# Graph transformer stack on one core: VectorE by hand, deferred statistics, bursts of two or three

## The chip, the cores and the metric

The kernel runs on one core of a Trainium2 chip. The core has five engines with an instruction queue each: TensorE (PE in the profile, its weight loads PEld), VectorE (DVE), ScalarE (ACT), GpSimd (POOL) and SyncE (SP), which issues most DMAs. The metric is the device time of one execution in microseconds (us).

## What is computed

Sixteen graphs of 1024 nodes with 128 features share one adjacency matrix. Three layers of masked attention with eight heads of 16, each followed by a feed-forward part of 256, and a last layer of graph attention with one head. All is float32.

```python
def layer(x):                       # L0, L1, L2: own weights each
    Q, K, V = (h @ Wq), (h @ Wk), (h @ Wv)          # 8 heads of 16
    scores = einsum('bnhd,bmhd->bhnm', Q, K) / sqrt(HEAD_DIM)
    scores = where(adj == 0, -inf, scores)
    attn = softmax(scores, axis=-1)
    attn_out = einsum('bhnm,bmhd->bnhd', attn, V).reshape(B, N, OUT_DIM)
    x = layer_norm(h + (attn_out @ Wo + bo), ln1_g, ln1_b)
    y = relu(x @ W1 + b1) @ W2 + b2
    return layer_norm(x + y, ln2_g, ln2_b)

def last(x):                        # L3
    h = x @ W
    e = leaky_relu((h @ a_src)[:, :, None] + (h @ a_dst)[:, None, :], 0.2)
    att = softmax(where(adj == 0, -inf, e), axis=-1)
    return layer_norm(einsum('bij,bjd->bid', att, h) + x)
```

(Names and numbers of dimensions are shortened; x has 16 x 1024 x 128 values here as the kernel asserts it.)

## The kernel before

**Blocks, steps, pairs.** A block is one graph in one of the three attention layers: 48 blocks, four graphs taken in turn through the layers (`LANES`). A block has 32 steps: two groups of four heads, two halves of 512 queries, eight tiles of 128 keys. A step has two pairs; a pair is the scores of two heads of one tile of keys against 512 queries, 128 x 1024 values in one of three slots `s` of PSUM (two banks each). One bank `t` is for all other products, one, `acc`, for the sums of probabilities and values.

**A pair's way.** TensorE computes the scores (L428). On DVE's way (`on_dve`, L436) VectorE adds the mask on the way out of PSUM (L438) and ScalarE takes the exponential in SBUF one burst later (L473), two pairs in one instruction where they lie side by side. On POOL's way (`on_pool`, L441) ScalarE takes the exponential out of PSUM (L443) and GpSimd multiplies by a mask of zeros and ones (L444). `av_step` (L479) multiplies the probabilities by the values into `acc`; after eight steps `finish` transposes the sums on VectorE into `tt` (L490), takes a reciprocal (L492), and GpSimd scales into `A` (L493).

**Bursts.** The main loop (L836) takes three pairs at a time: `burst` puts the outer two on DVE's way and the middle one on POOL's, in every sixteenth burst all three on DVE's (`POOL_RESTS`). An operation of the graph layer's edges (`fill`, L634, with its VectorE operation L645) makes a burst with one pair on POOL's way. After the burst's scores come: one piece, the exponentials of the burst before, the sums of steps that are three bursts old (`AHEAD`), and a second piece.

**Pieces.** All other work stands in chains of tasks, with the tiles each takes and gives back: the projections of the next block (`proj_tasks`: two transpositions `t0`, four `split`, which leave a rounded part on ScalarE, L392, and the rest on VectorE, L393, and two `v`), what follows a block's attention (`post_tasks`: `gather`, `out_proj`, `x1t`, `ffn1`, `ffn2`), and the graph layer (`last_tasks`: `xt`, `nodes`, `rows_gh`, four times `edges` and `aggregate`, `end`). `AT` gives the step of a block from which each piece of a projection or post chain is due; others are due some steps after the one before. `piece` takes the first due one. `need` forces pieces that must be done. A projection or an FFN product is emptied from `t` on VectorE (L336) and followed by statistics of four tiles (L329, L331) and by GpSimd's normalisation (L344 to L348).

**Who sets the order.** In the main loop TensorE's and ScalarE's instructions stand in the order of the program (`manual_schedule`). VectorE's, GpSimd's and SyncE's stand where a list scheduler puts them by a model of costs; `soon` raises the priority of some evacuations. Each engine then runs its queue in that order, with waits on semaphores. After the last block the remaining chains are run off in the loop at L872.

Of the kernel before, what the change touches and what calls it, by code (L numbers as in the profile page):

```python
# [32 lines left out]
AT = {"proj": (1.5, 4.5, 9, 10.5, 12, 15, 16.5, 18), "post": (13.5, 19.5, 21, 22.5, 24, 25.5, 27, 28.5, 30, 39.5)}  # L33
AT_END = {3: (13.5, 19.5, 21, 22.5, 24, 25.5, 27, 28.5, 30, 31.5), 2: (7.5, 9, 12, 13.5, 15, 16.5, 18, 19.5, 21, 22.5)}
AHEAD = 3
BURST = 3
POOL_RESTS = 16
# [79 lines left out]
def fast_path(ctx: ExitStack, tc: tile.TileContext, a: dict, out: bass.AP, flag):  # L117
# [169 lines left out]

    def transpose_half(name, src, h, gain=None, bias=None):
# [44 lines left out]
    def add_and_stats(n):  # L333
        def out(ts, ps):
            with soon():
                nc.vector.tensor_add(n[0][:, ts, :], v3(ps), n[0][:, ts, :])  # L336
            stats(n, ts)
        return out
# [24 lines left out]

    def proj_tasks(m):
# [4 lines left out]
        def t0(h):  # L369
            def run():  # L370
                x = state["x", b]
                if l == 0:
# [10 lines left out]
        def split(n, h):  # L383
            def run():
# [6 lines left out]
                with soon():  # L391
                    nc.scalar.copy(hi[:, c], ps)  # L392
                    nc.vector.tensor_sub(lo[:, c], ps, hi[:, c].bitcast(F32))  # L393
            return run
# [8 lines left out]
        pieces = [t0(0), t0(1), split("Wk", 0), split("Wq", 0), split("Wk", 1), split("Wq", 1), v(0), v(1)]  # L403
        return [(2 if n in (3, 4, 5, 6) else 1, f, {0: "+w", 1: "+w", 6: "-w", 7: "-w"}.get(n, "")) for n, f in enumerate(pieces)]
# [42 lines left out]
    e_of, masked, bursts = {}, [], [0]  # L447

    def burst(edge, pairs):

        old = list(masked)
        masked.clear()
        if edge is not None:
            edge()
            on_pool(*pairs[0], e_pair())
        else:
            e, ep = e_tile(), e_pair()
            rests = bursts[0] % POOL_RESTS == POOL_RESTS - 1 or len(pairs) < BURST
            for i, pair in enumerate(pairs):
                if i == 1:  # L460
                    (on_dve if rests else on_pool)(*pair, ep)
                else:
                    on_dve(*pair, e[:, i:i + 2, :])
            masked.append(e[:, 0:2 * ((len(pairs) + 1) // 2)])
            if rests and len(pairs) > 1:
                masked.append(ep)
            bursts[0] += 1
# [14 lines left out]
    def finish(g, qh, acc):  # L482

        def run():
# [4 lines left out]
            with soon():  # L489
                nc.vector.transpose(tt.rearrange("p a b -> p (a b)"), acc)  # L490
            rec = state["recs"][:, g, qh, :]
# [6 lines left out]
    def post_tasks(b, l):  # L498
# [4 lines left out]
        def gather(h):  # L503
            def run():
                s["aT", h] = half_tile("aT")
                nc.vector.transpose(s["aT", h], att[:, h].rearrange("p k g d -> p (k g d)"))
                if h == 1:
                    check_range(recs.rearrange("p g h k -> p (g h k)"))
            return run

        def out_proj(h):
            def run():
                if h == 0:
                    s["n1"] = with_stats(state["x", b])
                project([s["aT", h]], [w["Wo"]], h, add_and_stats(s["n1"]))
                normalise(s["n1"], slice(4 * h, 4 * h + 4))
            return run

        def x1t(h, alone=False):
            def run():  # L520
                x1 = s["n1"][0]
# [16 lines left out]
        def ffn2(h):  # L538
            def run():
# [4 lines left out]
                normalise(s["n2"], slice(4 * h, 4 * h + 4))  # L544
# [31 lines left out]
    def last_tasks(b):  # L576
# [3 lines left out]
        def xt(h):  # L580
            def run():
                w = W[L - 1]
                if h == 0:
# [70 lines left out]
        def aggregate(u):  # L654
            def run():
# [13 lines left out]
                stats(s["n"], slice(2 * u, 2 * u + 2))  # L669
                if u % 2:  # L670
                    normalise(s["n"], slice(2 * u - 2, 2 * u + 2))
                if u == 3:
                    check_range(s["col"].rearrange("p c t -> p (c t)"))
            return run

        def end():
            y = s["n"][0]
# [54 lines left out]

    def piece():
# [35 lines left out]
    def av_next():  # L769
# [7 lines left out]
        if left[half] == 0:  # L777
            m, g, qh = half
            b, l = blocks[m]
            while g == 0 and qh == 0 and last_attn:  # L780
                need(last_attn.pop())
            finish(g, qh, sums)()
# [51 lines left out]
    with tc.manual_schedule(engines={mybir.EngineType.PE, mybir.EngineType.Activation}):  # L834
# [278 lines left out]
```

## Time and profile before

| what | us |
|---|---|
| median of three runs | 4096.12 (4089.81 to 4096.95) |
| the profiled execution | 4093.11 |
| its span, first to last instruction | 4091.3 |
| mask additions on VectorE, 2074 | 2423.4, 1211 ns each |
| multiplications on GpSimd, 998 | 2008.6, 2026 ns each |
| exponentials in SBUF on ScalarE, 1068 | 1989.8 |
| exponentials out of PSUM on ScalarE, 998 | 1027.2, 1029 ns each |
| products with the values on TensorE | 1545.7 |
| scores on TensorE | 1096.2 |

A row of a list of groups gives line, engine, operation, tiles and shapes, count, busy time, mean time of one in ns, and the idle time of the engine just before these instructions with what ended it. A row of waits gives the waiting instruction, what released it, the sum in us, how often, and the longest. A row of the timeline gives start, duration in us, engine, line, operation, tiles and count of merged instructions; in brackets the idle time before.

### The profile page before, as it was taken

The page shows a single profiled execution, that of the slowest core. Times are in us where ns is not written, and L with a number is a line of the kernel's source. Part 1 is how long each engine was busy: PE and PEld are TensorE (multiplying, and loading weights), DVE is VectorE, ACT ScalarE, POOL GpSimd, SP SyncE. Part 2 cuts the span into 40 slices and gives each one's busy share as a digit, 9 for nine tenths or more (in the row PEclk, how much of TensorE's full clock was granted, in tenths as well). Part 3 has the DMA queues.
Part 4 walks back from the last instruction along what each step waited for, and adds up shares of the span by engine and source line. Part 5 has one row for each costly group of instructions (what it writes and reads, how often), then busy time and mean ns, then how long its engine had stood idle before and what let it go on. Part 6 is the DMA issues. An engine that isn't in the chain of part 4 may idle for free.

```text
span 4091.3 us, 106755 instructions
## 1 busy us (share of the span) xinstructions
PE 3695.3 (90%) x44501; PEld 1620.2 (40%) x44501; DVE 3335.9 (82%) x5288; ACT 3285.3 (80%) x2955; POOL 3403.7 (83%) x3048
## 2 busy tenths in 40 slices
PE   6999999989989999998888999999989899999885
PEld 2333333344443333334444333333444433333444
DVE  6888988877778989886777898988777788989853
ACT  6899999977669999996666999999767799999740
POOL 4788989878879989887877988988888789989873
PEclk8999999999999999999999999999999999999997
DMA  6222222212212222211222222222122122222100
GB/s 153 68 63 50 55 63 63 63 46 54 56 45 70 55 57 63 63 47 50 53 54 54 63 56 50 63 63 61 48 62 54 48 63 53 55 60 63 43 10 16
DMA packets 124458, 233.06 MB, mean 57 GB/s; under 512 B 34625, under 2 KB 73793, under 8 KB 123969
## 3 DMA queue, kind: packets, MB, share of 16 engines
q1 hardware_dynamic: 123056, 225.74, 21.9%
q8 instruction: 354, 5.80, 0.6%
q14 instruction: 136, 1.11, 0.1%
q10 hardware_dynamic: 912, 0.42, 0.0%
HBM read 15.54 MB, written 8.39 MB: 6 GB/s over the span
## 4 chain that ended last, share of the span: by engine, by line
PE 42%; DVE 36%; POOL 10%; issue 5%; ACT 4%; SPq 1%; DMA 0%; DVEq 0%; ACTq 0%; POOLq 0%
DVE e L438 21%; PE acc L479 15%; PE t L304 14%; PE s L428 9%; POOL e L444 4%; DVE st L329 3%; DVE e L645 2%; DVE x L336 2%; POOL x L352 2%; ACT e L473 2%; PE t L293 2%; POOL x L353 2%; DVE lo L393 2%; DVE tt L490 2%; ACT e L443 1%
## 5 line engine op out<-in xcount | busy, mean ns | idle before, releaser
L438 DVE TENSOR_TENSOR e<-s,mask_add 128x1024 f32<-128x1024 f32 x2074 | 2423.4, 1211 | 386.5 <-PE s L428 370.0
L444 POOL TENSOR_TENSOR e<-e,mask 128x1024 f32<-128x1024 f32 x998 | 2008.6, 2026 | 397.7 <-ACT e L443 388.2
L473 ACT ACTIVATE e<-e 128x2048 f32<-128x2048 f32 x1068 | 1989.8, 1873 | 1.3 <-DVE e L438 1.3
L479 PE MATMUL acc<-e,v 128*17 128x512 f32 x12288 | 1545.7, 601 | 62.8 <-DVE tt L490 48.8
L443 ACT ACTIVATE e<-s 128x1024 f32<-128x1024 f32 x998 | 1027.2, 1029 | 420.1 <-PE s L428 346.6
L428 PE MATMUL s<-Wq,Wk 64*128 64x512 f32 x6144 | 1096.2, 443 | 169.6 <-DVE e L438 96.5
L428 PEld LDWEIGHTS s<-Wq,Wk 64*128 64x128 f32 x6144 | 512.4, 185 | 1142.4 <-DVE e L438 562.4
L479 PEld LDWEIGHTS acc<-e,v 128*17 128x17 f32 x12288 | 315.5, 98 | 690.8 <-issue 602.8
L348 POOL TENSOR_SCALAR x<-x,mv 128x128 f32<-128x128 f32 x896 | 389.2, 448 | 23.4
L352 POOL TENSOR_TENSOR x<-x,ln_g 128x1024 f32<-128x1024 f32 x97 | 229.5, 2366 | 51.9 <-PE t L293 47.0
L346 POOL TENSOR_TENSOR mv<-mv,half_neg 128x4 f32<-128x4 f32 x224 | 232.4, 1037 | 18.6
L304 PE MATMUL t<-hd,e 128*32 128x129 f32 x7040 | 208.6, 275 | 13.7 <-DVE lo L393 11.4
L304 PE MATMUL t<-x1T,W 128*32 128x512 f32 x1520 | 203.6, 607 | 15.0 <-DVE parts L622 5.7
L304 PEld LDWEIGHTS t<-hd,e 128*32 128x32 f32 x7040 | 194.4, 110 | 49.1 <-DVE lo L393 30.1
L329 DVE BATCH_NORM_STATS2 st<-x 128x6 f32<-128x128 f32 x896 | 196.8, 279 | 4.1
L304 PE MATMUL t<-W,hT 128*32 128x128 f32 x6080 | 187.2, 276 | 0.3 <-DVE x L667 0.3
L344 POOL TENSOR_SCALAR mv<-mv 128x4 f32<-128x4 f32 x224 | 52.9, 236 | 156.0 <-DVE mv L331 103.5
L304 PEld LDWEIGHTS t<-W,hT 128*32 128x32 f32 x6080 | 162.0, 110 | 34.3 <-issue 24.9
L645 DVE SCALAR_TENSOR_TENSOR e<-s,mask 128x1024 f32<-128x1024 f32 x128 | 151.8, 1201 | 26.7 <-PE s L642 26.7
L535 ACT ACTIVATE hT<-t,b 128x512 f32<-128x512 f32 x190 | 132.5, 697 | 43.9 <-PE t L304 43.8
L392 ACT CAST hi<-t 128x512 fp32r<-128x512 f32 x188 | 110.3, 587 | 63.4 <-PE t L304 62.2
L293 PE MATMUL t<-identf,x 128*128 128x128 f32 x876 | 144.4, 288 | 18.7 <-DVE lo L393 9.0
(120 smaller groups left out, 2547.7 us busy)
## 6 DMA issues: line engine op xcount, KB each, us to landing
Wk<-hi SPq DMA_DIRECT2D x384, 128.0 KB
Wk<-lo SPq DMA_DIRECT2D x384, 128.0 KB
Wq<-hi SPq DMA_DIRECT2D x384, 128.0 KB
Wq<-lo SPq DMA_DIRECT2D x384, 128.0 KB
x<-in_x_dram SPq DMA_DIRECT2D x16, 512.0 KB
out_dram<-x SPq DMA_DIRECT2D x31, 256.0 KB
ai<-in_adj_dram SPq DMA_DIRECT2D x8, 512.0 KB
g_rows<-parts SPq DMA_DIRECT2D x124, 4.0 KB
```

The costliest lines, as they stand in the source:

```text
L304: nc.tensor.matmul(dst[j:j + SLOT, :], lhsT[:, j:j + SLOT], rhs, start=start, stop=stop)
L329: nc.vector.bn_stats(st[:, t, :], z[:, t, :])
L346: nc.gpsimd.tensor_tensor(v, v, half_neg[:, ts], OP.pow)
L348: nc.gpsimd.tensor_scalar(z[:, t, :], z[:, t, :], mv[:, t, 0:1], mv[:, t, 1:2], op0=OP.add, op1=OP.mult)
L352: nc.gpsimd.tensor_mul(z, z, rows(gain, n))
L428: nc.tensor.matmul(ps[:, r * 512:(r + 1) * 512], k[64 * r:64 * r + 64, kt * P:(kt + 1) * P], q[64 * r:64 * r + 64, qh * 512:(qh + 1) * 512 ...
L438: behind["dve"] = nc.vector.tensor_add(ev, psv, mask_of(mask_add, step)).ins
L443: nc.scalar.activation(ev, psv, AF.Exp, scale=HD ** -0.5)
L444: behind["pool"] = nc.gpsimd.tensor_mul(ev, ev, mask_of(mask01, step)).ins
L473: nc.scalar.activation(ev, ev, AF.Exp, scale=HD ** -0.5)
L479: nc.tensor.matmul(acc[j * SLOT:j * SLOT + HD + 1, :], v_bufs[m % 2][:, kt, 2 * j + g, :], e[j // 2][:, j % 2, :], start=first, stop=last)
L645: nc.vector.scalar_tensor_tensor(e[:, c:NT:2, :], ps.rearrange("p (j q) -> p j q", q=256), 1.0, mask01[:, c:NT:2, u * 256:(u + 1) * 256], ...
```

## The change

VectorE's instructions of the main loop get the order of the program too. Statistics of the norms, in items of two tiles (0.87 us by the program's own account), and the gathers' transpositions go to a list `later`; `use_spare` at the end of a burst takes from it while the burst's account stays within `SPARE`, or while more than `MANY` wait. `settle` runs what a later step needs. GpSimd's normalisation is put into the list behind its statistics. The second call of the piece runner in a burst is taken out, and a burst has two pairs instead of three while two pieces are due (`due_now`). Which pairs go POOL's way is set by a running credit of 0.3125 per pair. The projections' pieces come in another order, values first, and `AT` and `AT_END` have other steps. The diff is shown without lines around it.

```diff
@@ -33,2 +33,2 @@
-AT = {"proj": (1.5, 4.5, 9, 10.5, 12, 15, 16.5, 18), "post": (13.5, 19.5, 21, 22.5, 24, 25.5, 27, 28.5, 30, 39.5)}
-AT_END = {3: (13.5, 19.5, 21, 22.5, 24, 25.5, 27, 28.5, 30, 31.5), 2: (7.5, 9, 12, 13.5, 15, 16.5, 18, 19.5, 21, 22.5)}
+AT = {"proj": (4.5, 6, 7.5, 10.5, 13.5, 15, 16.5, 18), "post": (19.5, 22.5, 25.5, 27, 28.5, 30, 32, 33.5, 35, 41)}
+AT_END = {3: (12, 15, 18, 19.5, 21, 22.5, 24, 25.5, 27, 30), 2: (7.5, 9, 12, 13.5, 15, 16.5, 18, 19.5, 21, 22.5)}
@@ -37 +37,3 @@
-POOL_RESTS = 16
+POOL_SHARE = 0.3125
+SPARE = 0.9
+MANY = 3
@@ -287,0 +290,22 @@
+    later, used = deque(), [0.0]
+    def postpone(key, cost, f):
+        if head[0] or tail[0]:
+            f()
+        else:
+            later.append((key, cost, f))
+    def settle(key):
+        while any(k == key for k, _, _ in later):
+            later.popleft()[2]()
+    def use_spare():
+        while later and (used[0] + later[0][1] <= SPARE or len(later) > MANY):
+            _, cost, f = later.popleft()
+            f()
+            used[0] += cost
+            if len(later) <= MANY and used[0] > SPARE:
+                break
+        used[0] = 0.0
@@ -337 +361,4 @@
-            stats(n, ts)
+            used[0] += 0.69
+            for t in range(ts.start, ts.stop, 2):
+                postpone(id(n), 0.87, lambda t=t: stats(n, slice(t, t + 2)))
+            postpone(id(n), 0.0, lambda: normalise(n, ts))
@@ -363,0 +391,2 @@
+    ready = {}
@@ -371,0 +401,2 @@
+                if ("x", b) in ready:
+                    settle(id(ready["x", b]))
@@ -393,0 +425 @@
+                used[0] += 0.69
@@ -403,2 +435,2 @@
-        pieces = [t0(0), t0(1), split("Wk", 0), split("Wq", 0), split("Wk", 1), split("Wq", 1), v(0), v(1)]
-        return [(2 if n in (3, 4, 5, 6) else 1, f, {0: "+w", 1: "+w", 6: "-w", 7: "-w"}.get(n, "")) for n, f in enumerate(pieces)]
+        return [(1, t0(0), "+w"), (1, t0(1), "+w"), (1, v(0), ""), (1, v(1), ""), (1, split("Wk", 0), ""),
+                (1, split("Wq", 0), "-w"), (1, split("Wk", 1), ""), (1, split("Wq", 1), "-w")]
@@ -447 +479 @@
-    e_of, masked, bursts = {}, [], [0]
+    e_of, masked, credit = {}, [], [0.0]
@@ -452,0 +485,2 @@
+        credit[0] += POOL_SHARE * len(pairs)
+        pool = len(pairs) // 2 if credit[0] >= 1 else None
@@ -455,13 +489,17 @@
-            on_pool(*pairs[0], e_pair())
-        else:
-            e, ep = e_tile(), e_pair()
-            rests = bursts[0] % POOL_RESTS == POOL_RESTS - 1 or len(pairs) < BURST
-            for i, pair in enumerate(pairs):
-                if i == 1:
-                    (on_dve if rests else on_pool)(*pair, ep)
-                else:
-                    on_dve(*pair, e[:, i:i + 2, :])
-            masked.append(e[:, 0:2 * ((len(pairs) + 1) // 2)])
-            if rests and len(pairs) > 1:
-                masked.append(ep)
-            bursts[0] += 1
+        if pool is not None:
+            credit[0] -= 1
+        left_pairs = [i for i in range(len(pairs)) if i != pool]
+        e = e_tile() if left_pairs and (len(pairs) > 1) else None
+        ep = e_pair() if pool is not None or len(pairs) == 3 or e is None else None
+        places = [e[:, 0:2, :], e[:, 2:4, :]] if e is not None else []
+        if ep is not None and pool is None:
+            places.insert(len(pairs) // 2, ep)
+        for i, pair in enumerate(pairs):
+            if i == pool:
+                on_pool(*pair, ep)
+            else:
+                on_dve(*pair, places.pop(0))
+        if e is not None:
+            masked.append(e[:, 0:min(4, 2 * (len(left_pairs) - (pool is None and len(pairs) == 3)))])
+        if ep is not None and pool is None:
+            masked.append(ep)
@@ -490,0 +529 @@
+            used[0] += 0.95
@@ -504,2 +543 @@
-            def run():
-                s["aT", h] = half_tile("aT")
+            def dve():
@@ -508,0 +547,5 @@
+            def run():
+                s["A"] = att
+                s["aT", h] = half_tile("aT")
+                postpone(id(att), 0.8, dve)
@@ -514,0 +558 @@
+                settle(id(s["A"]))
@@ -516 +559,0 @@
-                normalise(s["n1"], slice(4 * h, 4 * h + 4))
@@ -520,0 +564 @@
+                settle(id(s["n1"]))
@@ -544 +588 @@
-                normalise(s["n2"], slice(4 * h, 4 * h + 4))
+                ready["x", b] = s["n2"]
@@ -582,0 +627 @@
+                settle(id(ready["x", b]))
@@ -669,5 +714,9 @@
-                stats(s["n"], slice(2 * u, 2 * u + 2))
-                if u % 2:
-                    normalise(s["n"], slice(2 * u - 2, 2 * u + 2))
-                if u == 3:
-                    check_range(s["col"].rearrange("p c t -> p (c t)"))
+                used[0] += 0.87
+                def rest():
+                    stats(s["n"], slice(2 * u, 2 * u + 2))
+                    if u % 2:
+                        normalise(s["n"], slice(2 * u - 2, 2 * u + 2))
+                    if u == 3:
+                        check_range(s["col"].rearrange("p c t -> p (c t)"))
+                postpone(id(s["n"]), 0.87, rest)
@@ -676,0 +726 @@
+            settle(id(s["n"]))
@@ -732,0 +783,5 @@
+    def due_now():
+        return sum(1 for chain in chains for n, q in enumerate(chain["queue"])
+                   if (q[4] is not None and q[4] <= now[0]) or (n == 0 and is_due(chain)))
@@ -781,0 +837 @@
+                settle(id(state["A"]))
@@ -834 +890 @@
-    with tc.manual_schedule(engines={mybir.EngineType.PE, mybir.EngineType.Activation}):
+    with tc.manual_schedule(engines={mybir.EngineType.PE, mybir.EngineType.Activation, mybir.EngineType.DVE}):
@@ -838 +894 @@
-            take_n = 1 if edge else min(BURST, 2 * len(steps) - p)
+            take_n = 1 if edge else min(BURST if due_now() < 2 else 2, 2 * len(steps) - p)
@@ -843,0 +900 @@
+            old = burst(edge, pairs)
@@ -845,7 +902,3 @@
-                with tc.manual_schedule(engines={mybir.EngineType.DVE}):
-                    old = burst(edge, pairs)
-                    t = late.popleft()
-                    neighbours(t)
-                    masks(t, mask_rows(t))
-            else:
-                old = burst(edge, pairs)
+                t = late.popleft()
+                neighbours(t)
+                masks(t, mask_rows(t))
@@ -864 +917 @@
-            piece()
+            use_spare()
@@ -870,0 +924,3 @@
+            use_spare()
+        while later:
+            later.popleft()[2]()
```

## The prediction

> **What bounds the kernel now.** I read the page first, then two stretches of the span cut out with their busy times, then the list of PE's own waits, then the timeline.
>
> ```profile
> span 4091.3 us, 106755 instructions
> PE 3695.3 (90%) x44501; PEld 1620.2 (40%) x44501; DVE 3335.9 (82%) x5288; ACT 3285.3 (80%) x2955; POOL 3403.7 (83%) x3048
> PE 42%; DVE 36%; POOL 10%; issue 5%; ACT 4%; SPq 1%; DMA 0%; DVEq 0%; ACTq 0%; POOLq 0%
> ```
>
> PE and DVE hold 78% of the chain that ended last; PE is idle for 4091.3 - 3695.3 = 396 us. These are the two kinds of stretch (columns: window, its length, then busy us of PE, PEld, DVE, ACT, POOL, clock, DMA share, GB/s), three blocks of attention alone and three blocks in which the graph layer's pieces run too, and then the tail:
>
> ```profile
> 1405.20:1623.30 218.10, 204.94 (x2160) 80.66 (x2160) 193.54 (x290) 201.00 (x171) 193.84 (x169) 0.99 0.24 59
> 1959.60:2277.00 317.40, 276.10 (x3934) 135.11 (x3934) 231.32 (x405) 209.00 (x200) 247.06 (x233) 0.97 0.21 52
> 3963.40:4091.30 127.90, 77.56 (x1616) 63.09 (x1614) 45.37 (x135) 6.56 (x27) 51.03 (x70) 0.75 0.06 16
> ```
>
> In a plain stretch PE is 94% busy, with 13.2 us idle in 218.1; in a graph stretch 87%, with 41.3 us idle in 317.4. The other engines have more idle time in both. So what can be won is PE's idle time, and the list of its waits says who ends it:
>
> ```profile
> PE s L428 <- DVE e L438: 96.5, 166, 2.1
> PE acc L479 <- DVE tt L490: 48.8, 50, 2.2
> PE s L428 <- DVE e L645: 27.5, 36, 1.4
> PE t L304 <- DVE lo L393: 22.6, 23, 2.0
> ...
> PE t L304 <- DVE hd L610: 17.4, 20, 1.5
> ...
> PE t L293 <- DVE lo L393: 9.0, 10, 1.5
> ```
>
> There are two kinds. Scores (L428) wait for a slot that a late mask addition (or an edge operation, L645) still reads: 96.5 + 27.5 = 124.0 us. Pieces (L304, L293) wait for the single bank t that the piece before has not been emptied from: 22.6 + 9.0 + 17.4 and eleven smaller rows of the same list (DVE parts 5.7, ACT v 3.7, ACT x1T 3.6 and 1.2, DVE hd 3.6, DVE x 3.5 and 2.1, ACT hT 2.7, 1.8 and 1.1, ACT xT 1.9) make 79.9 us. How the first kind arises:
>
> ```profile
> 1487.89 0.47 DVE L329 BATCH_NORM_STATS2 st<-x 128x6 f32<-128x128 f32 x2
> ...
> 1488.28 0.36 DVE L331 BATCH_NORM_AGGREGATE mv<-st 128x2 f32<-128x6 f32 x4
> 1488.56 1.19 DVE L438 TENSOR_TENSOR e<-s,mask_add 128x1024 f32<-128x1024 f32 x1
> ...
> 1489.66 0.68 DVE L393 TENSOR_TENSOR lo<-t,hi 128x512 fp32r<-128x512 f32 x1
> 1489.76 0.73 PE L428 MATMUL s<-Wq,Wk 64*128 64x512 f32 x4
> 1490.26 3.48 DVE L438 TENSOR_TENSOR e<-s,mask_add 128x1024 f32<-128x1024 f32 x3
> ...
> 1491.62 0.49 PE L428 MATMUL s<-Wq,Wk 64*128 64x512 f32 x2 [1.13 <-DVE e L438]
> ```
>
> Statistics and an evacuation stand before mask additions; PE then waits 1.13 us for a slot. (This burst also has three additions, as every sixteenth has, and that stays.)
>
> **The change, part by part.** *Counts.* By the order of the two built programs the mask additions on DVE go from 2074 to 2112 and POOL's multiplications from 998 to 960: DVE gets 38 x 1.211 = 46 us, POOL loses 38 x 2.026 = 77 us. In blocks of attention alone the share is the same (15 bursts in 16); the 38 fall into graph blocks and the head and tail, where DVE is idle for 317.4 - 231.3 = 86 us in three blocks. Cost nothing while that cover lasts, 46 us without it. Exponentials: 1006 of two pairs become 932, 62 of one pair become 248, ACT's from PSUM 998 become 960: 186 x 1.049 - 74 x 1.924 - 38 x 1.029 = +14 us on ACT, hidden by ACT's 108 us of idle time in a graph stretch, where the bursts of two lie; 14 us without it.
>
> *Statistics one item per burst, DVE in program order.* I priced the two orders of DVE: between one mask addition and the next, the sum of everything else on DVE (four statistics 0.87 and four aggregates 0.36 by the timeline, transposition of sums 0.71, reciprocal 0.23, x 0.68, lo 0.68, edge 1.19, by their groups). A burst of 3.41 us (64 in the 218.1 us) has two additions of 1.21, so about 1.0 us is free for such work; what a run has above 1.0 us delays the next addition. Summed over all runs this excess is 446 us before and 276 us after; runs over 1.6 us fall from 261 to 156. If slot waits go with the excess, 124.0 us falls to 124.0 x 276/446 = 76.7: a gain of 47 us. Bounds: all 124 gone, or none, because part of the waits are for bursts with three additions. I take 47.
>
> *One piece per burst.* The second call of the piece runner goes, and bursts of two appear where two pieces are due: 811 bursts of three, 293 of two, against 996 to 1006 of three. Bursts that hold two or more pieces in the main part fall from 133 to 40 of them, so pieces that follow each other in the bank t have scores or sums between them: 79.9 x (1 - 40/133) = 56 us gained. Bounds: 0 and 80.
>
> *More bursts.* About 97 more. No row prices a burst by itself; the nearest is the wait of scores for an addition, 96.5/166 = 0.58 us, met in 166 of 1050 bursts. Bounds: below nothing, since a burst of two leaves a slot free for the next burst (-0.58 each, -56 us), to one such wait in each (+56). I take the rate of today, 97 x 166/1050 x 0.58 = 9 us lost.
>
> *Waits added.* In program order an item whose input is late holds the additions behind it, and PE behind these. The items are the transposition of sums (48.8 us of PE's waits today; its place behind PE's own last sum stays, bounds -49 to +49, taken as 0), the gather, which waits for POOL's A, and the evacuation, which waits for its piece. The evacuation comes right behind its burst's additions and before the next burst's scores exist, so it holds nothing. The gather is a rival below.
>
> *Order of pieces, due times.* The values first, then keys and queries: the last split is due at step 18 and its DMAs are issued at step 21 as before; they have 11 steps, about 25 us, to land. SP's queue keeps its 1928 instructions. Taken as 0; if the stacks came late, the first scores of 47 blocks would wait, which today costs 8.0 us in all (row Wk<-hi of PE's waits).
>
> *Tail.* 127.9 us, PE idle for 50.3 us, now with DVE by hand: its order is already that of PE's aggregates. Taken as 0, bounds -10 and +10 from the 19.5 us for which PE waits there for L645.
>
> **The sum** is made against the profiled execution: 4093.1 us (span 4091.3 and 1.8 around it), 3.0 below the median of 4096.12. 4093.1 - 47 - 56 + 9 = 3999; I say **4000 us**, 2.3% less.
>
> **A rule against it.** The page's matmul row says 90%. The Trainium skill, Perfetto Trace Analysis, section Identifying the Most-Contended Engine, holds that matmul busy time is not a fair measure because matmuls are pipelined, and that one should go by weight loads, and by occupancy for the others. By it PE (PEld 40%) is not the limit and ACT, 201 of 218 us in a plain stretch, is; then nothing is won by shorter waits of PE, and the added 14 us make 4107. The chain speaks for the row: ACT has 4% of it, PE and DVE 78%, and ACT's idle time there is ended by PE.
>
> **The rivals.** *A, slower: DVE stands at a late gather.* L506 waits for POOL's A; today 20 such waits cost DVE 32.6 us, 1.6 on the mean, 5.6 at most, with additions put ahead of it where the scheduler saw the wait. With the order fixed each of 48 blocks can meet it, and POOL, 89% busy in a plain stretch, has normalisations (0.24 + 0.23 + 1.04 + 1.74 = 3.3 us) in its queue at that time. At 5.6 us a block, 48 x 5.6 = 269 us: 3999 + 269 = 4268; at 3 us, 4143. It decides from 94/48 = 2.0 us a block. For it: POOL has 10% of the chain. Against: the item is put off by up to three bursts, about 10 us.
>
> *B, little won.* Slots are also held by ACT's exponentials, and ACT has 17 us of slack in 218; only the pieces' waits go: 4093 - 56 + 14 = 4051.
>
> *C, more won.* In graph blocks the engines run dry behind long pieces (DVE waits 148.7 us for L304 ahead of L664); bursts of two also halve the 41.3 us of idle time per three graph blocks: 16/3 x 20.6 = 110 in place of 56, and slot waits go wholly: 4093 - 110 - 124 + 9 = 3868; half the way from 4000 is 3934.
>
> *D, no difference:* the excess returns at forced settlements (53 runs over 3 us are left, of 82): 4096.
>
> **How the numbers follow.** Forecast (3960 to 4040) 0.43; B (4040 to 4087) 0.17; C (under 3960) 0.13; D 0.06; A 0.21. About 0.2% is what a measurement of this kernel can tell from no change. Faster 0.73, same 0.06, slower 0.21. The likeliest case's own range is 3960 to 4040. The range for 8 in 10 reaches into C to 3900 and past D into A to 4120; below it lies some 0.05, above 0.15.
>
> **What would show it.** In the profile after: the rows of PE waiting for additions and L645 at 77 us together, those for the bank t at 24 us; PE 92% busy; runs of four statistics gone from DVE between additions; a plain stretch of three blocks near 212 us, a graph stretch near 295. Wrong if DVE's wait ahead of the gather passes 100 us (A), if ACT's share in a plain stretch rises above 95% with the time as before (B), or if the waits for slots stay at 124 us.

## The result, and the profile after

The changed kernel takes **4190.07 us** in the median of four runs (4188.54 to 4197.22) beside 4094.49 us for the kernel before (4089.81 to 4096.95, four runs): a ratio of 1.0238, 95% interval 1.0221 to 1.0256. It is slower by 96 us; the forecast was 4000 us.

The page of the profile after, its span and its busy times:

```profile
span 4187.8 us, 106949 instructions
PE 3753.6 (90%) x44501; PEld 1601.3 (38%) x44501; DVE 3422.1 (82%) x5326; ACT 3294.3 (79%) x3029; POOL 3330.8 (80%) x3010
```

PE is idle for 4187.8 - 3753.6 = 434 us, 38 more than before, and busy for 58 us more with the same 44501 matmuls. The clock records of the trace hold 255.5 us at half clock (a granted TensorE clock of 0.5), 196.3 before. By estimate, if a stretch at half clock loses half its work, these 59 us more account for up to 30 of the 58; what lengthens the matmuls by the rest is not shown. The chain of waits on this page ends in a stretch of GpSimd without going back, so it is not used; the stretches and PE's waits answer in its place. The same three kinds of stretch as in the prediction (window, length, busy us of PE, PEld, DVE, ACT, POOL, clock, DMA share, GB/s): three plain blocks, three graph blocks, the tail:

```profile
1450.40:1671.50 221.10, 206.39 (x2164) 79.67 (x2160) 196.34 (x290) 201.66 (x171) 193.97 (x169) 0.99 0.23 58
1992.20:2322.40 330.20, 285.76 (x3958) 135.24 (x3958) 245.00 (x414) 212.57 (x220) 231.14 (x224) 0.96 0.21 53
4061.10:4187.70 126.60, 80.08 (x1888) 66.02 (x1888) 54.23 (x162) 8.24 (x29) 60.12 (x89) 0.79 0.06 16
```

The plain stretch is 3.0 us longer, the graph stretch 12.8 us, the tail the same. Who ends PE's idle time after (waiting instruction, releaser, sum in us, times, longest):

```profile
PE acc L517 <- DVE tt L528: 85.6, 75, 2.7
PE s L460 <- DVE e L470: 72.2, 161, 1.0
PE t L317 <- DMA x<-in_x_dram: 43.4, 6, 7.6
PE acc L517 <- POOL mv L373: 21.4, 8, 2.7
PE acc L517 <- POOL e L476: 18.0, 18, 1.9
PE s L460 <- DMA Wq<-lo: 17.6, 2, 12.9
PE t L328 <- DVE lo L424: 17.6, 36, 1.7
...
PE s L460 <- DVE e L690: 15.6, 36, 0.6
...
PE t L317 <- DVE hd L655: 8.6, 7, 1.3
PE t L328 <- DVE hd L655: 7.7, 8, 1.1
```

(L517 was L479, L528 was L490, L460 and L470 were L428 and L438, L690 was L645, L317 and L328 were L293 and L304.) The two kinds of wait at which the change aimed did fall: scores for a slot from 124.0 to 72.2 + 15.6 = 87.8 us, pieces for the bank `t` from 79.9 to 41.3 us (the `lo` and `hd` rows and seven small ones). Others took their place: the sums wait for the transposition `tt` 85.6 us in place of 48.8, for GpSimd's `mv` and `e` 39.4 in place of 11.3, a load of x is waited for six times, 43.4 us, and one wait of 12.9 us stands in the head.

The timeline shows the load of x (start, duration, engine or queue, line, operation; the idle time before in brackets):

```profile
959.27 0.39 SPq L731 DMA_DIRECT2D out_dram<-x  x1
959.77 0.70 SPq L673 DMA_DIRECT2D g_rows<-parts  x1
960.52 0.62 SPq L674 DMA_DIRECT2D h_rows<-parts  x1
...
969.80 0.60 SPq L674 DMA_DIRECT2D h_rows<-parts  x1
970.44 0.44 SPq L158 DMA_DIRECT2D x<-in_x_dram  x1
...
974.90 1.09 PE L317 MATMUL t<-identf,x 128*128 128x128 f32 x4 [7.20 <-DMA x<-in_x_dram]
```

SP issues sixteen transfers of rows, 0.6 to 0.7 us each, ahead of the next graph's load of x, which PE uses 4.5 us after its issue; PE stands for 7.2 us. Before, the load stood in front of the rows in all places; after, behind them in six. And a late transposition in a plain stretch:

```profile
1616.54 0.30 DVE L355 BATCH_NORM_AGGREGATE mv<-st 128x2 f32<-128x6 f32 x2
...
1616.76 1.27 DVE L544 STREAM_TRANSPOSE aT<-A 128x512 f32<-128x512 f32 x2
...
1617.96 0.30 DVE L387 TENSOR_REDUCE chk<-recs 128x1 int32<-128x64 int32 x2
1618.18 0.70 DVE L528 STREAM_TRANSPOSE tt<-acc 128x512 f32<-128x512 f32 x1
...
1618.94 1.91 PE L517 MATMUL acc<-e,v 128*17 128x512 f32 x16 [1.16 <-DVE tt L528]
```

In the order of the program the put-off items (statistics, the gather's `aT`, the checks of the reciprocals) come ahead of `tt`, for which PE waits; nobody waits for `aT` at that moment. Over all 75 such waits, VectorE's time between PE's last sum and `tt` goes to mask additions and edges 68 us, to `aT` 42, to statistics and aggregates 37 and to checks 12; in the 50 waits before, it is 45 us of additions and edges and under 1 us of anything else (worked out from the traces).

### The profile page after: what moved, and what is told of

The parts are those of the page before. It is cut to its first block, busy times and chain, and to the rows that moved or that the text cites. A ratio compares the mean times of both kernels' runs of the same rounds, so it can differ in the third digit from the quotient of the medians.

```text
span 4187.8 us, 106949 instructions
## 1 busy us (share of the span) xinstructions
PE 3753.6 (90%) x44501; PEld 1601.3 (38%) x44501; DVE 3422.1 (82%) x5326; ACT 3294.3 (79%) x3029; POOL 3330.8 (80%) x3010
## 5 line engine op out<-in xcount | busy, mean ns | idle before, releaser
L470 DVE TENSOR_TENSOR e<-s,mask_add 128x1024 f32<-128x1024 f32 x2112 | 2474.7, 1212 | 505.8 <-PE s L460 452.2
L476 POOL TENSOR_TENSOR e<-e,mask 128x1024 f32<-128x1024 f32 x960 | 1933.5, 2025 | 552.3 <-ACT e L475 540.2
L511 ACT ACTIVATE e<-e 128x2048 f32<-128x2048 f32 (+1 forms) x1180 | 2046.2, 1744 | 8.8 <-DVE col L709 7.6
L517 PE MATMUL acc<-e,v 128*17 128x512 f32 x12288 | 1585.3, 606 | 125.6 <-DVE tt L528 85.6
L475 ACT ACTIVATE e<-s 128x1024 f32<-128x1024 f32 x960 | 990.1, 1031 | 485.3 <-PE s L460 380.6
L460 PE MATMUL s<-Wq,Wk 64*128 64x512 f32 x6144 | 1124.2, 450 | 130.4 <-DVE e L470 72.2
L460 PEld LDWEIGHTS s<-Wq,Wk 64*128 64x128 f32 x6144 | 509.6, 187 | 1242.6 <-DVE e L470 529.4
L517 PEld LDWEIGHTS acc<-e,v 128*17 128x17 f32 x12288 | 313.8, 98 | 738.6 <-issue 558.5
L379 POOL TENSOR_TENSOR x<-x,ln_g 128x1024 f32<-128x1024 f32 (+1 forms) x97 | 229.6, 2367 | 20.3 <-PE t L317 19.7
L317 PE MATMUL t<-identf,x 128*128 128x128 f32 x868 | 164.6, 298 | 70.2 <-DMA x<-in_x_dram 43.4
L328 PE MATMUL t<-hd,e 128*32 128x129 f32 x6912 | 204.6, 275 | 10.3 <-DVE lo L424 7.7
L328 PE MATMUL t<-x1T,W 128*32 128x512 f32 x1520 | 203.4, 605 | 2.2 <-DVE parts L667 1.4
L328 PEld LDWEIGHTS t<-hd,e 128*32 128x32 f32 x6912 | 189.4, 110 | 30.3 <-DVE lo L424 12.6
L328 PE MATMUL t<-W,hT 128*32 128x128 f32 x5952 | 181.7, 274 | 0.6 <-DVE x L360 0.5
L328 PEld LDWEIGHTS t<-W,hT 128*32 128x32 f32 x5952 | 156.8, 110 | 32.1 <-issue 28.7
L528 DVE STREAM_TRANSPOSE tt<-acc 128x512 f32<-128x512 f32 x192 | 136.3, 710 | 30.7 <-PE acc L517 29.0
L317 PEld LDWEIGHTS t<-identf,x 128*128 128x128 f32 x868 | 96.6, 144 | 167.9 <-issue 105.1
L690 DVE SCALAR_TENSOR_TENSOR e<-s,mask 128x1024 f32<-128x1024 f32 x128 | 149.0, 1207 | 7.5 <-PE s L687 7.5
```

The costliest lines, as they stand in the source:

```text
L317: nc.tensor.transpose(ps[:, t * P:(t + 1) * P], src[:, 4 * h + t, :], identf)
L328: nc.tensor.matmul(dst[j:j + SLOT, :], lhsT[:, j:j + SLOT], rhs, start=start, stop=stop)
L379: nc.gpsimd.tensor_mul(z, z, rows(gain, n))
L460: nc.tensor.matmul(ps[:, r * 512:(r + 1) * 512], k[64 * r:64 * r + 64, kt * P:(kt + 1) * P], q[64 * r:64 * r + 64, qh * 512:(qh + 1) * 512 ...
L470: behind["dve"] = nc.vector.tensor_add(ev, psv, mask_of(mask_add, step)).ins
L475: nc.scalar.activation(ev, psv, AF.Exp, scale=HD ** -0.5)
```

## The experiments

Each kernel is measured beside the kernel before on the same chip, whose median was 4092.1 to 4096.2 us. "Blocks" below are cut at the last transposition of sums of each block; this table is worked out from the traces (us; the 26 plain and 18 graph blocks between the first and last two, half = us at half clock):

```
kernel               plain 26   graph 18   half
before               1891.5     1686.8     196
after                1917.1     1749.0     256
a_fetchprio          1916.9     1694.5     208
a_fixed              1917.2     1698.8     187
a_fixed_tt           1865.7     1691.3     169
a_fixed_nodefer      1931.4     1675.6     239
a_sched_head         1905.3     1631.0     182
a_sched_nodefer      1901.0     1636.4     155
a_sched_2p           1904.2     1724.6     275
a_sched_oldorder     1892.1     1677.2     180
b_neworder           1944.9     1716.4     310
b_tt                 1868.3     1665.4     200
a_sched_nodefer_tt   1871.0     1633.9     148
```

**1. The load of x in front of the rows** (`a_fetchprio`; the first load of the head, which `fetch(1)` made, is written out without it):

```diff
-            state["x", b] = load_x(b)
+            with tc.high_priority(offset=2000):
+                state["x", b] = load_x(b)
```

> The kernel after, with one thing changed: the loads of the next graph's x get a high priority, so that in SyncE's queue they stand behind one of the sixteen DMAs of a graph layer's rows and not behind all of them (in five of eleven places). Theory LATE LOAD (the loss lies in these loads: six waits of TensorE of 7.2 us, 43 us, and TensorE's half clock after each, some 8 us more of matmul time in each of these blocks): the six waits shrink to under 2 us each, blocks of 115 us fall to about 102, the time falls by 60 to 90 us to 4100 to 4130. Theory FIXED ORDER (VectorE in program order holds the additions back): the blocks of 115 us stay above 110, the time falls by at most 43 us, to 4147 or more. Theory PIECES (one piece for each burst and the new due times leave the chain of the graph layer too late, whatever the queue): as FIXED ORDER, since the load is then held by the tile that is not free yet.

4136.67 us (1.0109, interval 1.0092 to 1.0126): 53 us less than the changed kernel. PE's waits for the load in the main loop are gone from the list, and the 54.5 us come out of the graph blocks. The time lies between the two ranges expected: the load's place on SP's queue is a cost of its own, and not the whole loss.

**2. VectorE left to the list scheduler** (`a_dvesched`, the changed kernel else; while the head still makes masks, VectorE's order stays by hand; names of engines shortened):

```diff
-    with tc.manual_schedule(engines={PE, Activation, DVE}):
+    with tc.manual_schedule(engines={PE, Activation}):
```

> The kernel after with VectorE's order in the main loop left to the list scheduler again, all else as after. Its queue of SyncE has no load of x behind the row DMAs. LATE LOAD: the plain stretch of three blocks stays at about 221 us, the graph blocks lose their peaks of 115 us, time 4100 to 4130. FIXED ORDER: the plain stretch falls to 218 us or less too, time about 4090 or less. PIECES: the plain stretch stays at 221 and the graph blocks keep most of their length, time above 4150.

4052.71 us, one execution. With this edit the load of x stands in front of the rows by itself, so it takes away two costs at once: 137 us, of which 53 are the load's by run 1.

**3. The order of pieces of before in the changed kernel** (`a_oldorder`: `AT`, `AT_END` and the projections' order put back):

> The kernel after with the order of pieces and the due times of before; VectorE in fixed order, deferred statistics, one piece for each burst and bursts of two stay. Its queue of SyncE has the loads of x ahead of the row DMAs, as before. LATE LOAD: peaks of 115 us gone, time 4100 to 4130. FIXED ORDER: no better than after but for the 43 us of waits, 4145 or more. PIECES: the plain stretch of three blocks comes back to 218 us or less and the time to 4090 or less.

4167.61 us, one execution. The load waits are gone here too, but a new row stands in PE's list:

```profile
PE acc L517 <- DVE tt L528: 82.4, 74, 5.3
PE t L328 <- DVE aT L544: 71.5, 31, 8.3
PE s L460 <- DVE e L470: 57.7, 123, 0.7
```

With the old due times the output projection waits for the put-off gather, up to 8.3 us. So the later due times belong to the deferral; they are what keeps this wait away in the changed kernel.

**4. VectorE in program order, alone, in the kernel before** (`b_dve`):

> The kernel before with one part of the change alone: VectorE's instructions of the main loop in program order, statistics right behind their addition as the program has them, two pieces for each burst, no bursts of two. FIXED ORDER: slower than before by 1% or more, 4135 to 4250, with more wait of TensorE for the transposition of the sums and for additions. LATE LOAD and PIECES: within 1% of before, 4055 to 4135, since neither the loads' place in the queue nor the due times differ from before.

4169.16 us, one execution: 77 us lost by this edit alone, with PE's waits for `tt` up from 48.8 to 73.0 us and no put-off items at all. These 24 us are not the whole: the waits for the bank `t` behind `lo` rise by 22 us (31.6 to 53.4), the waits for slots fall by 8, and PE is busy for 40 us more (3735.7 for 3695.3).

**5. The cut in the head** (`a_fixed`). Bursts of two shift the bursts against the blocks, so that in the changed kernel one burst holds pairs 47 and 48 of block 0. `before(24)`, called for pair 48, loads the stacks of keys and queries of the next block, and the scores of pair 47 (one of 3072) are then made from those: the changed kernel, and runs 1 and 2, compute this one pair from other data. In run 3 the bursts fall otherwise, and pairs 47 and 48 lie in two. PE waits for these loads:

```profile
103.43 1.65 PE L460 MATMUL s<-Wq,Wk 64*128 64x512 f32 x6 [12.90 <-DMA Wq<-lo]
```

Run 1 with one more line:

```diff
             take_n = 1 if edge else min(BURST if due_now() < 2 else 2, 2 * len(steps) - p)
+            if p < 48 < p + take_n:
+                take_n = 48 - p
```

> The kernel after with the early loads of x and one more change: no burst reaches over pair 48 of the first block. In the kernel after a burst holds pairs 47 and 48, the stacks of the next block are put in place of this block's when step 24 is prepared, and so the scores of pair 47 read the next graph's keys and queries and wait 12.9 us for their DMAs; here pair 47 reads its own. (The kernel after, and those of the first call but the one with the old order and the one made from before, compute this one pair of 3072 from the next block's keys and queries.) Expected if that is the whole of the wait: the first block 117 us in place of 131, the time 10 to 14 us below 4136.7, 4123 to 4127. If the wait only moves to the next use of these stacks: 4130 to 4137.

4128.45 us (1.0091, 1.0074 to 1.0108): 8 us less than run 1, where 10 to 14 were expected. All kernels of the changed kind from here on have this cut.

**6. The transposition ahead of the burst** (`a_fixed_tt`): where the next step of sums begins a new group after this burst, `av_next`, which finishes the old group with its transposition, is called before the burst's scores are made.

```diff
         while p < 2 * len(steps):
+            if len([w for w in waiting if w[1] <= number + 1 - AHEAD]) > 1 and left.get(waiting[0][0][:3]) == 1:
+                av_next()
```

> As a_fixed, and the eighth sum of a half, with the transposition of the sums behind it, is put ahead of a burst's scores and additions where another sum follows in the same burst, in place of behind them. Theory TRANSPOSITION LATE (what the fixed order costs is mostly TensorE's wait for the transposition, 85 us after against 49 before, because it stands behind two additions and the deferred items): that wait falls under 30 us, the plain stretch of three blocks from 221 to 218 us, the time by 40 to 60 us to 4065 to 4085. Theory COUPLING (the fixed order costs by many small waits of additions for evacuations and evacuations for pieces): the wait falls as much but others grow; the time falls by less than 20 us.

4071.18 us (0.9949, 0.9932 to 0.9965): 57 us less than run 5, 51.5 of them in the plain blocks. The wait for `tt` falls from 84.2 to 45.1 us, not to under 30 as expected: of VectorE's time ahead of `tt` in the 51 waits left, `aT` takes 54 us, statistics and aggregates 51, additions 22.

**7. The scheduled VectorE with the cut, and with both** (`a_sched_head` is run 2 with the cut; `a_sched_head_tt` adds the line of run 6):

> As the kernel after with VectorE left to the list scheduler, with pair 47 reading its own block's keys and queries. 4037 to 4043 if the head's wait of 13 us goes; 4053 if it only moves. Against a_fixed it gives the price of the fixed order alone, with the loads of x early in both: 80 to 90 us expected from the first call.

> As a_sched_head, with the eighth sum and its transposition ahead of the burst. TRANSPOSITION LATE: the scheduler puts the transposition early already (wait 46.6 us), so less is won than with the fixed order: 10 to 30 us, 4010 to 4030. COUPLING: within 10 us of a_sched_head.

4041.21 us (0.9878, 0.9861 to 0.9895) and **3998.47 us** (0.9776, 0.976 to 0.9792). The fixed order costs 4128.45 - 4041.21 = 87 us with the same items put off and the load early in both; and without it the change is a gain of 51 us, all in the graph blocks (1686.8 to 1631.0).

The line of run 6 wins 43 us here too, more than the 10 to 30 expected. So with that line in both, the fixed order still costs 4071.18 - 3998.47 = 73 us, and the late transposition is only a part of its price:

```profile
PE acc L518 <- DVE tt L529: 45.1, 51, 2.6
```

```profile
PE acc L517 <- DVE tt L528: 14.5, 20, 0.8
```

(`a_fixed_tt`, then `a_sched_head_tt`.) These rows account for 31 of the 73 us. PE is also busy for 38 us longer (3737.6 for 3699.8) at as much half clock (169 and 172 us); why its matmuls take longer there is not shown.

**8. Which part gains** (`a_sched_2p`: always three pairs and two pieces a burst; `a_sched_nodefer`: nothing put off), both from `a_sched_head`:

```diff
-            take_n = 1 if edge else min(BURST if due_now() < 2 else 2, 2 * len(steps) - p)
+            take_n = 1 if edge else min(BURST, 2 * len(steps) - p)
...
+            piece()
             use_spare()
```

```diff
-        if head[0] or tail[0]:
+        if True:
             f()
```

> The changed kernel with VectorE left to the scheduler and the cut at the end of the first 48 pairs (4041.2 us, graph blocks 1631.0 us in 18), but every burst of three and two pieces per burst as before; the deferral of the small items stays. If the gain of 51 us over the kernel before comes from one piece per burst (the waits of pieces for a bank), the time goes back to 4080 to 4095 us and the graph blocks to about 1680 us. If it comes from the deferral of the small items, the time stays within 10 us of 4041 us.

> The same kernel (4041.2 us) with nothing deferred: statistics and output transpositions run where their pieces stand; one piece per burst and the bursts of two stay. If the deferral counts for nothing where VectorE is scheduled anyway, the time stays within 10 us of 4041 us. If the deferral is the source of the gain in the graph blocks (1686.8 to 1631.0 us), the time goes to 4080 us or more and the graph blocks go back above 1675 us.

4137.67 us (1.0098, 1.0081 to 1.0115) and 4034.4 us (0.9856, 0.9837 to 0.9876). One piece a burst with bursts of two is worth 96 us here; that is more than the whole gain, and the time lies beyond the 4080 to 4095 expected, so something else in the change had to cost some 45 us. The deferral is worth nothing where VectorE is scheduled.

**9. The early transposition in the kernel before** (`b_tt`, the line of run 6 alone):

> The kernel before with one edit: where a group's last sum is due after the next burst, the group before it is finished, with its transposition on VectorE, ahead of the burst's scores instead of behind them. In the changed kernel this edit brought 57 us with the fixed order and 43 us with the scheduled one, all of it in the plain stretch and the first blocks. If the transposition's place is a cost of its own that the kernel before has too (48.8 us of its waits), it comes to 4045 to 4065 us, its plain stretch from 218.3 to about 215 us per three blocks. If the waits for it are a matter of the changed order of the pieces, it stays within 10 us of 4092 us.

4042.65 us (0.9873, 0.9856 to 0.989), 52 us less, by one line. The row of `tt`, 48.8 us before, is gone from PE's list, which now begins with these two:

```profile
PE s L428 <- DVE e L438: 103.5, 175, 1.6
PE s L428 <- DVE e L645: 25.8, 34, 1.3
```

**10. The order of pieces, and the deferral in a fixed order.** `b_neworder` is the kernel before with `AT`, `AT_END` and the projections' order of the changed one; `a_sched_oldorder` is `a_sched_nodefer` with those of before; `a_fixed_nodefer` is `a_fixed` with the edit of `a_sched_nodefer`.

> The kernel before with the changed order and due times of its pieces alone (keys and queries split last, later places for the chain behind a block); two pieces per burst, bursts of three, VectorE scheduled. If the 45 us by which the changed kernel with two pieces per burst stands behind the kernel before (4137.7 against 4092 us) are the new order's, this comes to 4125 to 4150 us. If the deferral made them, this stays within 10 us of 4092 us.

> One piece per burst and bursts of two while two pieces are due, with the order and due times of before, VectorE scheduled, nothing deferred. If one piece per burst is the source of the gain whatever the order, this comes to 4025 to 4050 us or less (with the new order: 4034.4 us). If one piece per burst pays only with the new order's places, where two pieces seldom fall due together, it comes to 4080 us or more.

> The changed kernel in fixed VectorE order with its head mended (4128.5 us), nothing deferred; the load of x then stands in front of the rows' transfers by itself. If the prediction's term for the deferral (47 us off the waits for score slots, in a fixed order) is right, taking the deferral out costs 30 us or more: 4155 to 4190 us. If the deferral brings nothing in a fixed order either, the time stays within 15 us of 4128 us.

`b_neworder`: 4167.25 us (1.0171, 1.0154 to 1.0188), slower than expected; `a_sched_oldorder`: 4077.76 us (0.9954, 0.9937 to 0.997), between the two expectations; `a_fixed_nodefer`: 4111.89 us (1.0037, 1.0023 to 1.0052), faster than `a_fixed` by 17 in the medians, just past the 15 allowed and on the other side of the predicted gain. So the new order alone costs 71 us and pays only with one piece a burst, which gains 18 us in the old order and 4167.25 - 4034.4 = 133 in the new. Why two pieces in the new places cost so much was not taken apart, but PE's list says where. `b_neworder`:

```profile
PE s L428 <- DVE e L438: 145.8, 204, 5.4
PE acc L479 <- DVE tt L490: 53.5, 46, 2.1
PE s L428 <- DVE e L645: 41.9, 43, 3.4
```

The waits for slots are 124.0 us before, 187.7 here, and 104.6 in `a_sched_nodefer` (96.9 below and 7.7 for the edges). The waits of pieces for the bank `t` (releasers `lo`, `hd`, `x`, `parts`, `v`, `x1T`, `hT`, `xT`; all rows, the smallest too) are 81, 61 and 53 us. So of the 133 us that one piece a burst gains, 83 are seen in the slots and 8 in the bank.

What a fixed order does is plainest without the deferral. PE's waits of `a_sched_nodefer`:

```profile
PE s L460 <- DVE e L470: 96.9, 152, 2.6
PE acc L517 <- DVE tt L528: 41.3, 39, 1.7
PE acc L517 <- DVE mv L355: 23.4, 18, 1.8
```

and of `a_fixed_nodefer`, whose lines stand one further down:

```profile
PE acc L518 <- DVE tt L529: 117.3, 84, 3.1
PE s L461 <- DVE e L471: 85.9, 177, 1.1
...
PE acc L518 <- POOL e L477: 6.4, 5, 2.7
```

The waits for `tt` rise by 76.0 us; the time rises by 4111.89 - 4034.4 = 77.5 in the medians and by 87 between the two profiled executions. That the first two agree is chance: other waits fall by 36 us, the waits for `mv` alone by 23, so that PE's idle time rises by 40 (337.4 to 377.2), and its busy time by 47, of which half clock (239 for 155 us) can make up to 42. Ahead of `tt`, additions and edges take 106 of some 175 us of VectorE's time, `aT` 23, statistics and aggregates 33. And what the deferral adds to that, in `a_fixed`:

```profile
PE acc L518 <- DVE tt L529: 84.2, 77, 2.6
PE s L461 <- DVE e L471: 72.4, 160, 1.0
PE acc L518 <- POOL mv L374: 24.1, 9, 2.7
PE acc L518 <- POOL e L477: 21.5, 19, 2.8
```

It takes 13.5 us off the waits for additions and 33.1 off those for `tt`, and brings 45.6 us of waits on GpSimd, of which 7.8 were there (1.4 and 6.4). Late statistics that make GpSimd's normalisation late, and its multiplications behind that, would do this; the order on GpSimd was not tested by itself. By these rows this is a gain of 9 us; by the time it is a loss of 17 in the medians and 9 between the two profiled executions (4120.6 and 4129.65). The plain blocks gain 14 us by it and the graph blocks lose 23. In the 18 graph blocks PE's waits for GpSimd's multiplications rise from 2.0 to 18.7 us and those for an x that GpSimd normalises from 0 to 6.4: together 23. In the plain blocks the waits for `tt` and additions fall by 45 and those for `mv` rise by 24.

**11. The best of both** (`a_sched_nodefer_tt`):

> The version of 4034.4 us (VectorE scheduled, one piece per burst, bursts of two, new order, nothing deferred) with the early transposition of the sums. If the two edits add up as they did with the deferral (43 us), it comes to 3985 to 4000 us, its plain stretch to about 215.5 us per three blocks. If the deferral is needed once the transposition no longer hides behind the scores, it stays above 4010 us.

4002.0 us (0.9761, 0.974 to 0.9782). It lies 2 us above the range expected for this case, below the 4010 of the other, and ties with `a_sched_head_tt` (3998.47): the deferral is not needed. PE's list has only 1.6 us left for `tt`.

**The account.** Pairs of kernels that differ by one part lead from the kernel before to the changed one:

```
new order of pieces, alone             4096.2 -> 4167.3    +71
one piece a burst, bursts of two       4167.3 -> 4034.4   -133
VectorE in program order               4034.4 -> 4111.9    +78
items put off                          4111.9 -> 4128.5    +17
no cut in the head                     4128.5 -> 4136.7     +8
load of x behind the rows              4136.7 -> 4190.1    +53
```

The second line also holds the new split of the pairs between the engines and the cut, which were not run alone. The steps add up in this order; in another order the same part can weigh otherwise, as one piece a burst does (18 or 133 us).

## Why the prediction was wrong

**The bound** was read rightly: shortening PE's waits is what pays, and the version of run 11 has PE's idle time at 4003.7 - 3694.5 = 309 us. The rule of the skill, as the prediction applied it, by which nothing would be won by shorter waits of PE, is not borne out: taking away 48.8 us of waits of PE brought 52 us (run 9). That section (Identifying the Most-Contended Engine) names two measures for TensorE, the matmul work done beside the peak and the weight loads; the prediction weighed only the second.

**The step that failed first** is in "Waits added": the transposition of sums, "its place behind PE's own last sum stays, bounds -49 to +49, taken as 0". It does not stay. The scheduler had left at most an addition in front of it; in program order whatever `finish` is emitted behind stands in front: additions of the burst, the gather's two transpositions, statistics and checks. The row rose from 48.8 to 85.6 us in the changed kernel, inside the bounds but not 0; between `a_sched_nodefer` and `a_fixed_nodefer`, where nothing is put off, it rose by 76.0, beyond the upper bound, which had come from doubling the 48.8 us. An early transposition alone won back 57 us (run 6). The fixed order as a whole cost 77 to 87 us, of which the prediction had none; with the early transposition in both kernels 73 us of it remain, and for these a cause is shown only in part (run 7). The row that was second in PE's list was the one to follow through the built program.

**The second** is in "Order of pieces, due times": "SP's queue keeps its 1928 instructions. Taken as 0." The count stayed and the order did not. The load of x went behind sixteen transfers, six times: +53 us, 43.4 of them as plain waits of PE. The step looked only at the stacks, whose loads were in time but for the head.

**The third** is the same "taken as 0" for the order itself: +71 us alone. It was hidden by one piece a burst.

**Statistics one item per burst**, a gain of 47 us, was wrong in its price. The measure it used did what was counted: the excess of VectorE's runs between additions over 1.0 us falls from 7.8 to 3.9 us per plain block between `a_fixed_nodefer` and `a_fixed`. The slot waits fell nearly as said (to 87.8, predicted 76.7), but mostly not by this item: in a fixed order the deferral takes them from 98.2 to 88.6 us, 10 us, where one piece a burst took 83 in the new order. That the sum came near is luck. And time did not follow: the deferral costs 17 us in a fixed order and gives nothing in a scheduled one. The excess says how long an addition is held up, not which instruction stands last in the run; that one was `tt`.

**One piece per burst**, a gain of 56 us: the size of what it and the new order gain together came out near, 133 - 71 = 62 us, 50 of them in the graph blocks, but the way did not. The waits for the bank `t` fell by 38.6 us in the changed kernel (predicted 56); yet where the part is taken alone, its gain stands in the waits for slots (83 us of 133, run 10) and only 8 us of it in the bank.

**More bursts**, 9 us, was not measured alone. **Counts** at no cost: additions on VectorE are 2112 and GpSimd's multiplications 960, as said; VectorE still has 330.2 - 245.0 = 85 us of idle time in three graph blocks. **Tail**: 127.9 to 126.6 us, as said.

**The head** had no step at all: 8 us by the cut, from a burst that straddles a load.

**The rivals.** A, slower at 4143 to 4268, held the time but not the cause: VectorE's wait for the gather's input, priced at 2.0 us a block and more, is one wait of 0.3 us after:

```profile
DVE aT L544 <- POOL A L532: 0.3, 1, 0.3
```

Its neighbour is real: PE waits for a late `aT` with the old due times (run 3, 71.5 us). B, C and D did not come about. Of the signs that were to show the prediction wrong none came (the gather's wait under 100 us, ScalarE at 201.66 of 221.10 us, slot waits below 124): each watched a wait that the prediction had priced, and the loss came by the waits it had set to zero.

## What to carry to other kernels

Before an engine's order is taken from a scheduler, list the instructions on it that another engine waits for, and place these first; the one line that did so for one of them here brought 52 us in the kernel before, where the whole change lost 96. Where a wait and the time change by the same amount, add up the other waits and the busy time too before the one is called the cause of the other. For a queue that issues transfers in order, compare the order of what is waited for against the bulk around it, not the number of instructions. A term set to zero wants its own look in the trace and in the built order, with the price of the case in which its cover is gone.

## What the runs showed of the hardware

The half clock of TensorE comes on a grid. In the traces of the kernel before, the changed one, `b_neworder` and `a_sched_nodefer_tt` every period at half clock begins on one grid of 3.413 us within its trace and lasts a whole number of its cells (29 of 37 periods before last one cell). Away from the head and tail, each cell in which PE was idle for more than 1.91 us in sum is followed by half clock, and no cell at full clock is followed by it with less than 0.58 us; between these both occur. (A cell that is itself at half clock was followed by another with as little as 0.33 us.) The gaps need not be long: in the kernel before, gaps of at most 1.3 us that add up to 2.2 us within 9 us stand ahead of several. By estimate a cell at half clock costs up to 3.413 / 2 = 1.7 us of work, so a wait of 2 us may cost nearly twice its length; the changed kernel's 59 us more at half clock are worth up to 30 us of its 96.

The Trainium skill, TensorE: Matmul & The Clock Gate, section Why this matters for your kernels, asks for no idle gaps over about 3 us between matmuls. That figure is near the 3.413 us of the grid; the condition is stricter here, since in the kernel before 1.85 us of idle time in one cell, in gaps of at most 1.01 us, was followed by half clock.

SP's issues can take longer than the load that stands behind them: sixteen transfers of rows held its queue for 970.44 - 959.77 = 10.7 us, while the load needed 4.5 us from issue to use.
